# 64x64 tiles in a small self attention, and a band built by base-4 digits

## The chip, the cores and the metric

The kernel runs on one core of a Trainium2 chip. The metric is the device time of one execution in microseconds. A profiled execution adds a trace, from which the times of single instructions below are taken.

## The reference

A Perceiver of four levels: 2 batches of 64 latents with 256 features, beside a context of 2 x 1024 rows with 192 features. Each level has a cross attention to the context, a mixing of the latents among themselves, and a mixture of experts, each with a layer norm in front and a residual. All is float32. Two of the twelve stages are touched by the change.

Level 0's self attention has 8 heads of 64 features and one key and one value head that all share. It normalises its input a second time with gain and bias, and normalises its output:

```python
# xn: (2, 64, 256); q: 8 heads of 64; k, v: one head of 64
q = (xn @ Wq) * 64 ** -0.5
k, v = split(xn @ Wkv)
p = softmax(q_h @ k.T)            # per batch and head, 64 x 64
out = layer_norm(concat_h(p @ v) @ Wo)
```

Level 1's mixing gives each latent t a softmax over 32 taps, computed from its own features, and sums that latent and the 31 behind it by these weights:

```python
w = softmax(x @ W.T + b)          # (2, 64, 32)
# out[t] = sum over taps k of w[t, k] * x[t + k], rows past the end left out
```

As a matrix this is a band of 64 x 64 for each batch: row t holds its 32 weights, moved to the right by t.

## The kernel before

All 2 x 64 latents lie on the 128 partitions (batch 0 on the first 64, batch 1 on the others), and a stage works on a tile `x` of 128 x 256. The stages follow one another. Matmuls of f32 appear in the trace as two records each. Within the edited stages the program order holds on TensorE (PE), VectorE (DVE), ScalarE (ACT) and GpSimd: `in_written_order` chains each engine's instructions as they are written. So PE does nothing in a wait unless other work is written there.

That other work is the fill. Generators such as `kv1.keys(b, c)` and `kv1.values(b, t)` project the keys and values that a later cross attention needs; `steps(fill[k], n)` runs n steps of one of them. A step is a few matmuls (two of 512 columns for keys by `ctxA` in L413 and `ctxB` in L418, or four of 256 for values in L387 and L389); the last step is the eviction from PSUM, on ACT (L480, L483). PSUM is split into two pairs of banks (`two_banks`) and four single banks (`bank`), each used in a ring.

**Level 0's self attention (L1207 to L1287).** `xlT` is the normalised input, transposed. `kT` holds the keys twice, on partitions 0 to 63 and 64 to 127. The queries are laid out so that one 128 x 128 matmul gives a head's scores of both batches, with zeros in `qx` that keep the two heads of a chunk apart:

```python
for h in range(8):
    nc.tensor.matmul(sc[:, h, :], qx[:, h // 2, h % 2, :], kT, start=True, stop=True)
```

Of each 128 x 128 result only the two blocks where query and key are of one batch are used. They are copied to `l0a_s` (DVE L1248, ACT L1249), go through a softmax there, and come into `p`, a tile of 128 x 1024 that is zero elsewhere. Eight transposes (L252), eight matmuls with `v` (L1263), the division by the sum (L1265), four transposes of the result `o` and four matmuls with `wo` follow. Then come the statistics (`bn_st`, L1276), the output norm and the residual. Level 0's expert stage starts with a layer norm, the rest of the fill and the transposes of `xl`.

**Level 1's mixing (L1529 to L1582).** After the softmax (exponentials in L1555, division in L1558 and L1559) the 32 weights of each row have to move to the right by the row's number. Six steps do it, one for each binary digit: `bits[:, k]` is 1 in the rows whose number has digit k set and `unset` is its opposite; a step adds the row as it is times `unset` (L1571) to the row moved by 2^k times `bits` (L1574). The last step writes into the two diagonal blocks of `band`. One transpose, a copy to `bandT`, one matmul with `xl` (L1580) and the residual (L271) end it. Three fill pairs (L387 and L389) stand ahead of the transpose, one behind the matmul.

Weights come over the SyncE queue in written order, each load as its buffer comes free.

Of the kernel before, what the change touches and what calls it, by code (L numbers as in the profile page):

```python
# [8 lines left out]
F32 = mybir.dt.float32  # L9
# [3 lines left out]
AF = mybir.ActivationFunctionType  # L13
ALU = mybir.AluOpType
AX = mybir.AxisListType
# [3 lines left out]
P = 128  # L19
D = 256  # L20
NB = 2
# [37 lines left out]
def tile_perceiver(ctx: ExitStack, tc: tile.TileContext, i: dict, out: bass.AP):  # L59
# [28 lines left out]
    def bank():  # L88
        return psum_now["b"].tile([P, 512], F32, tag="b", name="bank")

    def two_banks():
        return psum_now["a"].tile([P, 1024], F32, tag="a", name="two_banks")

    def stat(n=1, name="stat"):
        return small.tile([P, n], F32, tag=f"s{n}", bufs=12 if n == 1 else 4, name=name)
# [103 lines left out]
    for k in range(6, -1, -1):  # L199
        bit = bits[:, k : k + 1]  # L200
        nc.vector.tensor_scalar(bit, place, float(1 << k), None, ALU.is_ge)
        nc.vector.scalar_tensor_tensor(place, bit, -float(1 << k), place, ALU.mult, ALU.add)
    nc.vector.tensor_scalar(unset, bits, -1.0, 1.0, ALU.mult, ALU.add)
    iota8 = const.tile([P, 8], F32, name="iota8")
    nc.gpsimd.iota(
        iota8, pattern=[[1, 8]], base=0, channel_multiplier=0,
# [53 lines left out]
    def accumulate(dst, pairs):  # L260
        for k, (lhsT, rhs) in enumerate(pairs):
            nc.tensor.matmul(dst, lhsT, rhs, start=(k == 0), stop=(k == len(pairs) - 1))  # L262
# [104 lines left out]
    def features(xT, w, at, n):  # L367

        ps = bank()
        for f in range(n):  # L370
            accumulate(
                ps[:, f * P : (f + 1) * P],
                [(w[:, c, (at + f) * P : (at + f + 1) * P], xT[:, c, :]) for c in range(2)],
            )
        return ps
# [109 lines left out]
    def steps(work, n=9):  # L485

        for _, _ in zip(range(n), work):
            pass
# [719 lines left out]
    with psum(2, 4), stage_pool(name="l0a", bufs=1) as pool, in_written_order():  # L1208
        wq, wkv, wo = weight("l0a_wq"), weight("l0a_wkv"), weight("l0a_wo")
        xl = layernorm(x, twice=True, then=AF.Exp)  # L1210
        xlT = pool.tile([P, 2, P], F32, name="l0a_xT")

        qx = pool.tile([P, 4, 2, P], F32, name="l0a_qx")
        nc.gpsimd.memset(qx, 0.0)
        p = pool.tile([P, 8, P], F32, name="l0a_p")
        nc.gpsimd.memset(p, 0.0)
        base = tok.tile([P, D], F32, tag="xb", name="x_bias")
        nc.gpsimd.tensor_tensor(base, x, row("l0a_ob"), ALU.add)
        steps(fill[1], 2)
        ps = bank()  # L1220
        for c in range(2):
            nc.tensor.transpose(ps[:, c * P : (c + 1) * P], xl[:, c * P : (c + 1) * P], ident)
        for c in range(2):
            evacuate_affine(
                xlT[:, c, :], ps[:, c * P : (c + 1) * P], col("l0a_w", c), col("l0a_b", c)
            )

        ps = features(xlT, wkv, 0, 1)
        kT = pool.tile([P, P], F32, name="l0a_kT")
        nc.scalar.copy(kT, ps[:, :P])  # L1230
        ps = features(xlT, wq, 0, 4)
        for h in range(2):
            r = slice(h * S, (h + 1) * S)
            nc.vector.tensor_scalar(
                qx[r, :, h, :], ps[r, :].rearrange("p (c t) -> p c t", c=4), 0.125, None, ALU.mult
            )
        steps(fill[0])
        ps = bank()
        accumulate(ps[:, :64], [(xlT[:, c, :], wkv[:, c, P:]) for c in range(2)])
        v = pool.tile([P, 64], F32, name="l0a_v")  # L1240
        nc.vector.tensor_copy(v, ps[:, :64])
        steps(fill[1], 1)
        sc = two_banks().rearrange("p (h t) -> p h t", h=8)
        for h in range(8):
            nc.tensor.matmul(sc[:, h, :], qx[:, h // 2, h % 2, :], kT, start=True, stop=True)

        s = pool.tile([P, 8, S], F32, name="l0a_s")
        nc.vector.tensor_copy(s[0:S], sc[0:S, :, 0:S])  # L1248
        nc.scalar.copy(s[S:P], sc[S:P, :, S:P])  # L1249
        mx, tot = stat(8, "l0a_mx"), stat(8, "l0a_tot")  # L1250
        nc.vector.tensor_reduce(mx, s, AX.X, ALU.max)
        nc.vector.tensor_tensor(s, s, mx.unsqueeze(2).to_broadcast([P, 8, S]), ALU.subtract)
        for b in range(NB):
            r = slice(b * S, (b + 1) * S)
            nc.scalar.activation(p[r, :, r], s[r], AF.Exp)
        nc.vector.tensor_reduce(tot, p, AX.X, ALU.add)
        nc.vector.reciprocal(tot, tot)
        steps(fill[1])
        steps(fill[2], 3)
        pT = transposed(p.rearrange("p h t -> p (h t)"), 8, pool, "l0a_pT", "l0a_pT")  # L1260
        ps = bank()
        for h in range(8):
            nc.tensor.matmul(ps[:, h * 64 : (h + 1) * 64], pT[:, h, :], v, start=True, stop=True)  # L1263
        o = pool.tile([P, 512], F32, name="l0a_o")
        nc.vector.tensor_tensor(  # L1265
            o.rearrange("p (h d) -> p h d", h=8), ps.rearrange("p (h d) -> p h d", h=8),
            tot.unsqueeze(2).to_broadcast([P, 8, 64]), ALU.mult,
        )
        steps(fill[2])
        oT = transposed(o, 4, pool, "l0a_oT", "l0a_oT")  # L1270
        ps = bank()
        accumulate(ps[:, :D], [(oT[:, c, :], wo[:, c, :]) for c in range(4)])
        steps(fill[3], 1)

        st, mv = stat(6, "bn_st"), stat(2, "bn_mv")
        nc.vector.bn_stats(st, ps[:, :D])  # L1276
        nc.vector.bn_aggr(mv, st)
        r = stat(name="rstd")
        nc.scalar.activation(r, mv[:, 1:2], AF.Sqrt, bias=eps, scale=1.0)
        y = pool.tile([P, D], F32, name="l0a_y")  # L1280
        nc.vector.scalar_tensor_tensor(
            y, ps[:, :D], mv[:, 0:1], row("l0a_ow"), ALU.subtract, ALU.mult
        )
        nc.vector.reciprocal(r, r)
        x_new = xpool.tile([P, D], F32, tag="x", name="x_new")
        nc.vector.scalar_tensor_tensor(x_new, y, r, base, ALU.mult, ALU.add)
        x = x_new  # L1287
# [247 lines left out]
    with psum(2, 4), stage_pool(name="l1a", bufs=1) as pool, in_written_order():  # L1535
        steps(fill[1], 1)
        xl = layernorm(x, then=AF.Exp)
        xlT = turned_rows(xl)
        ps = bank()
        accumulate(ps[:, :32], [(xlT[:, c, :], router("l1a", c)) for c in range(2)])  # L1540
        steps(fill[1])
        steps(fill[2], 2)


        PAD = 32
        skew = [pool.tile([P, PAD + S], F32, name=f"l1a_skew{k}") for k in range(2)]
        for t in skew:
            nc.gpsimd.memset(t, 0.0)
        band = pool.tile([P, P], F32, name="l1a_band")
        nc.gpsimd.memset(band, 0.0)  # L1550
        w = skew[0][:, PAD : PAD + 32]
        nc.vector.tensor_tensor(w, ps[:, :32], row("l1a_b"), ALU.add)
        nm, tot, ri = stat(name="l1a_nm"), stat(name="l1a_tot"), stat(name="l1a_ri")
        nc.vector.tensor_reduce(nm, w, AX.X, ALU.max, negate=True)
        nc.scalar.activation(w, w, AF.Exp, bias=nm, scale=1.0, accum_out=tot)  # L1555
        steps(fill[2])
        steps(fill[3], 1)
        nc.vector.reciprocal(ri, tot)  # L1558
        nc.vector.tensor_scalar(w, w, ri, None, ALU.mult)  # L1559
        width = 32  # L1560
        for k in range(6):
            src, far = skew[k % 2], 1 << k
            width = min(width + far, S)
            if k < 5:
                places = [(slice(0, P), skew[1 - k % 2][:, PAD : PAD + width])]
            else:
                places = [
                    (r, band[r, r]) for r in (slice(b * S, (b + 1) * S) for b in range(NB))
                ]
            for r, dst in places:  # L1570
                nc.vector.tensor_scalar(  # L1571
                    dst, src[r, PAD : PAD + width], unset[r, k : k + 1], None, ALU.mult
                )
                nc.vector.scalar_tensor_tensor(  # L1574
                    dst, src[r, PAD - far : PAD - far + width], bits[r, k : k + 1], dst,
                    ALU.mult, ALU.add,
                )
        bandT = transposed(band, 1, pool, "bandT", "bandT")
        ps = bank()
        nc.tensor.matmul(ps[:, :D], bandT[:, 0, :], xl, start=True, stop=True)  # L1580
        steps(fill[3], 1)
        x = residual(x, ps[:, :D])  # L1582


    with psum(2, 4), stage_pool(name="l1f", bufs=2) as pool:
# [701 lines left out]
def layout(inputs):  # L2287
# [55 lines left out]
    a["l0a_wq"] = rows_first(g[p + "Wq"])  # L2343
    kv = g[p + "Wkv"]
    a["l0a_wkv"] = rows_first(np.concatenate([kv[:, :64], kv], axis=1))
    a["l0a_wo"] = rows_first(g[p + "Wo"])
    p = "L0_ffn_"
    a["l0f_w"] = np.concatenate(
        [flat(rows_first(g[p + "w1"])), flat(rows_first(g[p + "w2"]))], axis=-1
# [98 lines left out]
```

## Time and profile before

| | us |
|---|---|
| three runs | 691.6, 693.4, 694.55 |
| median | 693.4 |
| profiled execution | 693.79 |
| its span in the trace | 692.1 |
| level 0's self attention, from the end of the q matmuls to `bn_stats` | 85.2 to 103.2 |
| level 1's mixing, from the exponentials to the residual's end | 188.1 to 195.3 |
| mean granted TensorE clock over the span | 0.995 |

The time of an execution is 1.7 us longer than its span. In lines of the trace the first number is the start in us from the span's start (in groups: the busy time), then comes the busy time, engine, line and operation, what was written and read, and the shape; in brackets, how long the engine was idle before and what ended that. PEld is the weight load of TensorE, which overlaps with its matmuls. The ends of matmuls are modelled.

### The profile page before, as it was taken

The numbers are of one execution on the slowest core, as the hardware profiler recorded it, in microseconds if no ns is written. First come the engines' busy times: TensorE is split into PE (matmuls) and PEld (weight loads), VectorE is DVE, ScalarE is ACT, GpSimd is POOL, SyncE is SP. The second block draws the span as 40 slices with busy tenths as digits, with TensorE's granted clock in tenths as the row PEclk, the third lists the DMA queues.
The fourth block names the chain that finished last, engine by engine and source line by source line (L and its number), as shares of the span: only waits on it lengthen the run. The fifth ranks groups of instructions, "written<-read, shape, count | busy, mean of one in ns | idle before, by whom it ended". The sixth has DMA issues, their size and how long they took to land.

```text
span 692.1 us, 12000 instructions
## 1 busy us (share of the span) xinstructions
PE 654.6 (95%) x4956; PEld 513.6 (74%) x4956; DVE 297.7 (43%) x794; ACT 262.8 (38%) x531; POOL 64.4 (9%) x90
## 2 busy tenths in 40 slices
PE   7989979999989999999998989999999999999997
PEld 3547658866669988999997778899979966754443
DVE  5875333267540014555553435535322267643111
ACT  2463433288553333323322515305231168532111
POOL 3440100000100000000000040120000000000340
PEclk9999989999999999999999999999999999999999
DMA  8950004840018877000002300021138820368981
GB/s 284 412 232 1 19 36 138 298 142 2 2 62 290 306 247 252 1 2 1 1 1 67 116 0 1 2 65 59 62 108 295 292 97 2 111 270 341 390 317 54
DMA packets 21365, 93.07 MB, mean 134 GB/s; under 512 B 3056, under 2 KB 7680, under 8 KB 12512
## 3 DMA queue, kind: packets, MB, share of 16 engines
q1 hardware_dynamic: 19040, 85.96, 33.9%
q0 software_dynamic: 2016, 6.30, 2.5%
q8 instruction: 39, 0.64, 0.4%
q14 instruction: 14, 0.11, 0.1%
q10 hardware_dynamic: 256, 0.06, 0.0%
HBM read 98.46 MB, written 0.13 MB: 142 GB/s over the span
## 4 chain that ended last, share of the span: by engine, by line
PE 88%; DVE 7%; ACT 2%; issue 1%; DMA 0%; DVEq 0%; ACTq 0%
PE bank L262 30%; PE bank L1708 6%; PE two_banks L620 5%; PE two_banks L1657 4%; PE bank L665 3%; PE two_banks L1359 3%; PE two_banks L1664 3%; PE two_banks L1384 2%; PE two_banks L1903 2%; PE two_banks L387 2%; PE bank L1384 2%; PE bank L1429 2%; PE bank L2023 2%; PE two_banks L413 2%; PE two_banks L262 1%
## 5 line engine op out<-in xcount | busy, mean ns | idle before, releaser
L1708 PE MATMUL bank<-l2x_ctx,p 128*128 128x193 f32 x256 | 48.1, 327 | 0.0
L362 DVE SCALAR_TENSOR_TENSOR x_new<-bank,comb,x_new 128x256 f32<-128x256 f32 x24 | 11.6, 484 | 80.0 <-PE bank L262 80.0
L1708 PEld LDWEIGHTS bank<-l2x_ctx,p 128*128 128x128 f32 x256 | 40.8, 191 | 0.4
L1369 DVE CUSTOM_DVE_ANT_0 p<-two_banks,zero 128x1024 f32<-128x1024 f32 x32 | 38.6, 1217 | 5.1 <-PE two_banks L1359 5.1
L1377 ACT ACTIVATE p<-p,negmax 128x1024 f32<-128x1024 f32 x32 | 36.9, 1153 | 4.6 <-DVE negmax L1369 4.6
L1657 PE MATMUL two_banks<-l2x_qA,ctxA 128*128 128x128 f32 x256 | 31.9, 278 | 0.0
L1657 PEld LDWEIGHTS two_banks<-l2x_qA,ctxA 128*128 128x128 f32 x256 | 30.3, 192 | 1.1 <-issue 1.0
L1672 DVE TENSOR_REDUCE l2x_mx<-two_banks 128x128 f32<-128x1024 f32 x16 | 19.6, 1224 | 26.3 <-PE two_banks L1664 26.3
L1598 ACT ACTIVATE l1f_hT<-bank,cols 128x128 f32<-128x128 f32 x64 | 18.2, 368 | 32.9 <-PE bank L262 32.9
L262 PEld LDWEIGHTS bank<-xT,l1f_w_sb 128*128 128x128 f32 x256 | 29.7, 192 | 0.6 <-issue 0.3
L262 PE MATMUL bank<-xT,l1f_w_sb 128*128 128x128 f32 x256 | 30.1, 276 | 0.0
L262 PEld LDWEIGHTS bank<-xT,l2f_w_sb 128*128 128x128 f32 x256 | 29.6, 192 | 0.3
L262 PE MATMUL bank<-xT,l2f_w_sb 128*128 128x128 f32 x256 | 29.8, 275 | 0.0
L262 PE MATMUL bank<-l1f_w_sb,l1f_hT 128*128 128x256 f32 x128 | 28.8, 379 | 0.0
L1694 DVE TENSOR_TENSOR p<-two_banks,l2x_shift 128x512 f32<-128x512 f32 x32 | 20.6, 686 | 13.3 <-ACT l2x_shift L1689 13.3
L262 PEld LDWEIGHTS bank<-l1f_w_sb,l1f_hT 128*128 128x128 f32 x128 | 23.8, 190 | 2.9
L1701 ACT ACTIVATE p<-p 128x512 f32<-128x512 f32 x32 | 19.6, 630 | 12.1 <-DVE p L1694 12.1
L1384 PEld LDWEIGHTS two_banks<-ident,p 128*128 128x128 f32 x128 | 13.7, 141 | 10.9 <-ACT pT L1413 9.1
L620 PE MATMUL two_banks<-l3f_w_sb,m_xg 128*64 128x512 f32 (+1 forms) x112 | 21.2, 595 | 0.5 <-ACT m_xg L643 0.5
L215 ACT ACT_TABLE_LOAD x16 | 20.5, 1283 | 0.3
L628 DVE TENSOR_TENSOR m_prod<-two_banks,m_g 128x512 f32<-128x512 f32 x10 | 6.9, 690 | 31.1 <-PE two_banks L620 31.1
L1359 PE MATMUL two_banks<-n_kT,n_qx 32*128 32x512 f32 x128 | 19.2, 640 | 0.0
(580 smaller groups left out, 1356.5 us busy)
## 6 DMA issues: line engine op xcount, KB each, us to landing
l1f_w_sb<-in_l1f_w_dram SPq DMA_DIRECT2D x16, 1024.0 KB, 5.1
l3f_w_sb<-in_l3f_w_dram SPq DMA_DIRECT2D x12, 1024.0 KB, 6.0
more_w<-in_l3f_w_dram SPq DMA_DIRECT2D x12, 1024.0 KB, 10.9
l0f_w_sb<-in_l0f_w_dram SPq DMA_DIRECT2D x8, 1024.0 KB, 8.5
l2f_w_sb<-in_l2f_w_dram SPq DMA_DIRECT2D x8, 1024.0 KB, 4.8
l2f_w_sb<-in_l2f_w_dram SPq DMA_DIRECT2D x8, 512.0 KB, 4.7
xh<-in_ctx_dram SPq DMA_DIRECT2D x8, 192.0 KB, 6.0
l2x_ctx<-in_ctx_dram SPq DMA_DIRECT2D x1, 1536.0 KB, 7.8
```

Source lines behind the costliest of these rows:

```text
L215: nc.scalar.activation(junk, behind, func, scale=0.0)
L262: nc.tensor.matmul(dst, lhsT, rhs, start=(k == 0), stop=(k == len(pairs) - 1))
L620: nc.tensor.matmul(part[s], xg[r][:, c, s], shelf.at[r, j, n](c, f), start=False, stop=(c == 1), skip_group_check=True,)
L665: nc.tensor.matmul(ps[s, :D], hT[r][:, f, s], shelf.at[r, j, 2](f, slice(0, D)), start=(f == 0), stop=(f == last),)
L1359: nc.tensor.matmul(sc[u][:, n * 512 : (n + 1) * 512], qx[c, n][rows_, b].rearrange("p h q -> p (h q)"), kT[c, b][rows_, n, :], start=True, ...
L1369: nc.vector.tensor_tensor_reduce(p[u], sc[u], zero.to_broadcast([P, NK]), -1.0, 3.0e38, ALU.add, ALU.min, least)
L1377: nc.scalar.activation(p[u], p[u], AF.Exp, bias=sc[u], scale=-1.0, accum_out=total[u // 4][:, u % 4 : u % 4 + 1],)
L1384: nc.tensor.transpose(ps[:, kc * P : (kc + 1) * P], p[u][:, (4 * k + kc) * P : (4 * k + kc + 1) * P], ident,)
L1657: nc.tensor.matmul(sc[k][:, n, t, :], ctxA[:, b, n, t * P : (t + 1) * P], qA[:, j, b].rearrange("p h q -> p (h q)"), start=(t == 0), stop= ...
L1664: nc.tensor.matmul(sc[k][:, n, t, :], ctxB[half[n], b, t * P : (t + 1) * P], qB[half[n], j, b].rearrange("p h q -> p (h q)"), start=False, ...
L1694: nc.vector.tensor_tensor(p[k][:, n], sc[k][:, n], shifts[k].unsqueeze(1).to_broadcast([P, 4, P]), ALU.add,)
L1708: nc.tensor.matmul(po[k][:, : CD + 1], p[k][:, kc // 4, kc % 4, :], crows[:, b * 8 + kc, :], start=(kc == 0), stop=(kc == 7),)
```

## The change

In level 0's self attention the matmuls work on single 64 x 64 blocks: scores of one head and one batch, and the sum over values of one head and one batch. The queries stay as `features` gives them, in two halves. The values come onto four blocks (`v`, 128 x 128). Scores of the even heads go to one PSUM bank and those of the odd heads to another, so that the softmax needs no copy and is done in two halves of 128 x 256. The weights are divided by their sum before the transposes, one half on GpSimd and one on DVE. The matmul with `v` gives its result transposed already, so `o` and its transposes are gone; `wo`'s rows are reordered in the layout to suit. The memsets of `qx` and `p` are gone. Of the fill, `fill[1]`'s `ctxB` step stands behind the scores, `fill[2]`'s `ctxB` step behind `wo`, and its eviction behind the square root of the output norm.

In level 1's mixing rows move in three steps, one for each digit to the base of four: a multiplication of four shifted readings of the row with `digit` (products of `bits` and `unset`, made once at the start on GpSimd), and a reduction over the four. The blocks are turned by two 64 x 64 matmuls with `ident`; ACT and DVE copy one each into `bandT`. The division by the sum moves into the last addition. One of the three fill pairs moves behind the matmul with `xl`.

```diff
+    digit = const.tile([P, 3, 4], F32, name="digit")
+    low, high = (
+        [t[:, :6].rearrange("p (k u) -> p k u", u=2)[:, :, u] for t in (bits, unset)]
+        for u in range(2)
+    )
+    for j in range(4):
+        nc.gpsimd.tensor_tensor(digit[:, :, j], low[j % 2], high[j // 2], ALU.mult)
...
-        qx = pool.tile([P, 4, 2, P], F32, name="l0a_qx")
-        nc.gpsimd.memset(qx, 0.0)
-        p = pool.tile([P, 8, P], F32, name="l0a_p")
-        nc.gpsimd.memset(p, 0.0)
...
+        for j in range(2):
+            ps = features(xlT, wq, 2 * j, 2)
+            dst = qT[j].rearrange("p c t -> p (c t)")
+            if j == 0:
+                nc.vector.tensor_scalar(dst, ps[:, :D], 0.125, None, ALU.mult)
+                steps(fill[0])
+            else:
+                nc.scalar.activation(dst, ps[:, :D], AF.Identity, scale=0.125)
+        own = [slice(b * S, (b + 1) * S) for b in range(NB)]
         ps = bank()
-        accumulate(ps[:, :64], [(xlT[:, c, :], wkv[:, c, P:]) for c in range(2)])
...
+                    nc.tensor.matmul(
+                        ps[own[n], own[b]], xlT[:, c, own[b]], wkv[:, c, P:],
+                        start=(c == 0), stop=(c == 1),
+                    )
...
+        sc = [bank() for g in range(2)]
+        for c in range(4):
+            for b in range(NB):
+                for g in range(2):
+                    nc.tensor.matmul(
+                        sc[g][own[b], c * S : (c + 1) * S],
+                        qT[c // 2][own[g], c % 2, own[b]], kT[own[g], own[b]],
+                        start=True, stop=True,
+                    )
+        for g in range(2):
+            s, mx = sc[g][:, : 4 * S].rearrange("p (c k) -> p c k", c=4), stat(4, "l0a_mx")
+            nc.vector.tensor_reduce(mx, s, AX.X, ALU.max)
+            nc.vector.tensor_tensor(
+                p[g], s, mx.unsqueeze(2).to_broadcast([P, 4, S]), ALU.subtract
+            )
+            nc.scalar.activation(p[g], p[g], AF.Exp)
+        for g in range(2):
+            tot = stat(4, "l0a_tot")
+            nc.vector.tensor_reduce(tot, p[g], AX.X, ALU.add)
+            nc.vector.reciprocal(tot, tot)
+            engine = nc.vector if g else nc.gpsimd
+            engine.tensor_tensor(
+                weights[g], p[g], tot.unsqueeze(2).to_broadcast([P, 4, S]), ALU.mult
+            )
         steps(fill[1])
-        steps(fill[2], 3)
+        steps(fill[2], 2)
...
+            po = [bank() for n in range(2)]
+            for b in range(NB):
+                for n in range(2):
+                    nc.tensor.matmul(
+                        po[n][own[n], :D].rearrange("p (m t) -> p m t", m=2)[:, :, own[b]],
+                        v[own[n], own[b]], pT[g][own[n], :, own[b]], start=True, stop=True,
+                    )
+            nc.scalar.copy(oT[g][own[0]].rearrange("p m t -> p (m t)"), po[0][own[0], :D])
+            nc.vector.tensor_copy(oT[g][own[1]].rearrange("p m t -> p (m t)"), po[1][own[1], :D])
...
-        steps(fill[2])
-        oT = transposed(o, 4, pool, "l0a_oT", "l0a_oT")
...
+        steps(fill[2], 1)
         steps(fill[3], 1)
...
         nc.scalar.activation(r, mv[:, 1:2], AF.Sqrt, bias=eps, scale=1.0)
+        steps(fill[2])
...
+        for k, n in enumerate(steps_of):          # 1, 4, 16
+            width = min(width + 3 * n, S)
...
+            nc.vector.tensor_tensor(
+                terms, four, digit[:, k].unsqueeze(1).to_broadcast([P, width, 4]), ALU.mult
+            )
+            dst = rows_of if k == 2 else moved[k + 1][:, 12 * n : 12 * n + width]
+            nc.vector.tensor_reduce(dst, terms, AX.X, ALU.add)
...
+            nc.tensor.matmul(
+                turned[b][own[b], :S], rows_of[own[b]], ident[own[b], own[b]],
+                start=True, stop=True,
+            )
         nc.vector.reciprocal(ri, tot)
-        nc.vector.tensor_scalar(w, w, ri, None, ALU.mult)
...
-        steps(fill[3], 1)
-        x = residual(x, ps[:, :D])
+        steps(fill[3], 2)
+        x_new = xpool.tile([P, D], F32, tag="x", name="x_new")
+        nc.vector.scalar_tensor_tensor(x_new, ps[:, :D], ri, x, ALU.mult, ALU.add)
```

## The prediction

> **What bounds it now.** I read the page's 40 slices first, then the granted clock in short stretches, then the timeline of the two stages that are edited.
>
> ```profile
> PE   7989979999989999999998989999999999999997
> PEclk9999989999999999999999999999999999999999
> PE 88%; DVE 7%; ACT 2%; issue 1%; DMA 0%; DVEq 0%; ACTq 0%
> ```
>
> TensorE (PE) carries 88% of the chain that ended last and DMA none of it, so time comes off only where PE does less, or where PE idles. Both edits sit in such places: the sixth slice (86 to 104 us: busy 7, clock 8), and the eleventh and twelfth (173 to 208 us: busy 9 and 8). The list of waits names no DMA as what PE waited for, and weight loads start as buffers come free, so what is gained here should stay gained.
>
> ```profile
> 94.60:98.00 3.40, 2.27 (x19) 2.14 (x19) 0.98 (x2) 2.55 (x4) 0.00 (x0) 1.00 0.00 0
> 98.00:101.40 3.40, 2.62 (x9) 1.86 (x8) 0.69 (x1) 0.00 (x0) 0.00 (x0) 0.50 0.02 5
> 101.40:104.80 3.40, 3.40 (x9) 2.23 (x7) 1.41 (x5) 0.29 (x1) 0.00 (x0) 0.50 0.18 36
> ```
>
> In these stretches (busy time of PE, weight loads, DVE, ACT, POOL, then the clock) PE runs at half clock from 98.0 to 104.8 us, after a stretch of thin work. It is the only fall of the clock in this trace, and it doubles the matmuls by `wo`.
>
> ```profile
> 86.57 2.05 PE L1245 MATMUL two_banks<-l0a_kT,l0a_qx 128*128 128x128 f32 x16
> 88.66 0.68 DVE L1248 COPY l0a_s<-two_banks 64x512 f32<-64x512 f32 x1 [1.70 <-PE two_banks L1245]
> 89.37 0.58 ACT L1249 COPY l0a_s<-two_banks 64x512 f32<-64x512 f32 x1 [4.45 <-DVE l0a_s L1248]
> 89.99 0.69 DVE L1251 TENSOR_REDUCE l0a_mx<-l0a_s 128x8 f32<-128x512 f32 x1 [0.65 <-ACT l0a_s L1249]
> 91.49 1.28 ACT L1255 ACTIVATE l0a_p<-l0a_s 64x512 f32<-64x512 f32 x2 [1.54 <-DVE l0a_s L1252]
> 94.94 2.00 PE L1263 MATMUL bank<-l0a_v,l0a_pT 128*128 128x64 f32 x16 [0.87 <-DVE l0a_pT L103]
> 97.73 0.89 PE L252 MATMUL bank<-ident,l0a_o 128*128 128x128 f32 x4 [0.79 <-DVE l0a_o L1265]
> 99.40 3.78 PE L262 MATMUL bank<-l0a_wo_sb,l0a_oT 128*128 128x256 f32 x8 [0.79 <-DVE l0a_oT L103]
> 103.22 0.43 DVE L1276 BATCH_NORM_STATS2 bn_st<-bank 128x6 f32<-128x256 f32 x1 [3.87 <-PE bank L262]
> ```
>
> Level 0's attention is a serial chain: each row waits for the one above. From the end of the q matmuls (85.2) to the end of `wo` (103.2) it takes 18.0 us.
>
> **Level 0, part by part.** An f32 matmul is two records. Nothing in this trace has 64 rows and 64 columns of the array at once. The nearest rows:
>
> ```profile
> 74.54 0.45 PE L1097 MATMUL bank<-l0x_uT,l0x_wv 96*64 96x64 f32 x8
> 74.82 0.29 PE L1097 MATMUL bank<-pT,vl 128*64 128x64 f32 x4
> 75.04 1.12 PE L418 MATMUL two_banks<-ctxB,l1x_wk_sb 64*128 64x512 f32 x2
> ```
>
> Twelve records with halves of the columns in turn take 75.04 - 74.54 = 0.50 us, 42 ns each. Bounds: 34 ns (L1429, 32 records in 1.08 us) and 125 ns (L1263, 16 in 2.00 us). I take 42, as the shape is nearest, and 61 ns for the 16 records with 128 moving columns (half of L262's 1.95 us / 16 = 122 ns, two tiles in turn). After a group's last issue I add 0.2 us to its result.
>
> - Values: 16 records x 42 ns = 0.67, against 0.38 before; 85.2 to 85.9.
> - Scores: 32 x 42 = 1.34 + 0.2, done at 87.4. They now stand ahead of the fill (`ctxB`, 1.06 us) that ran before them. The second half of q is copied by ACT behind two 0.63 us key evictions (83.66 to 84.92), so at 85.6, before the scores need it.
> - Softmax on DVE: two times reduce and subtract at 0.42 (128x256: 0.415 in L1837, 0.425 in L1845), with gaps 1.85; 89.25. Both PSUM-to-SBUF score copies (0.68 + 0.58) are gone, and the exponentials (0.42 each) lie beside the other half's DVE work, apart from the last.
> - Sum 0.42, reciprocal 0.16, multiplication: GpSimd 0.72 (L1218's 0.723 for 128x256), about 1.4 with gaps: 90.65 for half 0; on DVE half 1 is ready at 91.0. Before, the sum over 1024 columns took 1.22, but beside PE.
> - PE meanwhile has 1.06 + 1.9 us of fill (`ctxB`, `ctxA`): 87.2 to 90.2, so it idles about 0.5. If that fill were not there, these 3 us would be idle and paid later.
> - Four transposes (0.13 each) in place of eight, evicted at 0.37 (ACT) and 0.42 (DVE): 91.9. ACT's two key evictions (1.26) come first, 89.7 to 90.9, just clear.
> - Weighing: 16 x 61 ns = 1.0, its first half overlapping the eviction: done 92.5. The copies of 64x256 (0.37 ACT, 0.42 DVE) end at 93.15 for half 1. The normalisation of the output (L1265, 0.69), the four transposes of `o` (0.89) and their copy (0.69) are gone.
> - `wo`: 2.1 us at full clock (L262's 1.13 for two matmuls, twice, less one drain), its first half ahead of the last copy: done at 94.8.
>
> So `bn_stats` starts at 94.8 instead of 103.2, 8.4 us earlier, of which 1.65 + 0.35 is the half clock on `wo` and on the transposes of `o`. After that PE holds the end, not the normalisation: fill of 1.06 (moved here) + 3.4 (two pairs of L387 and L389, 1.06 + 0.63 each) ends at 99.1, while `xl` is ready at 98.3 (3.5 us after `bn_stats`, as 106.7 - 103.2 before). The key eviction that now follows the square root on ACT (1.26 us) ends about when the next root needs ACT. The transposes of `xl` start at 99.1 instead of 107.14: **8.0 us**.
>
> The two memsets of 0.95 us on GpSimd stood off the path and give nothing. The four `digit` products on GpSimd are free: GpSimd is idle until 13.13 us, and `unset` is ready at 8.6. If that cover were gone they would cost about 0.6 (four at 0.14, L205's kind).
>
> **Level 1's mixing.**
>
> ```profile
> 188.54 0.16 DVE L1558 RECIPROCAL l1a_ri<-l1a_tot 128x1 f32<-128x1 f32 x1 [0.54 <-ACT l1a_skew L1555]
> 193.49 0.30 PE L252 MATMUL bank<-ident,l1a_band 128*128 128x128 f32 x1 [1.04 <-DVE l1a_band L1574]
> 194.18 0.70 PE L1580 MATMUL bank<-xl,bandT 128*128 128x256 f32 x2 [0.38 <-DVE bandT L103]
> 197.14 0.41 PE L252 MATMUL bank<-ident,xl 128*128 128x128 f32 x2 [0.77 <-DVE xl L238]
> ```
>
> From 188.54 to 193.34 DVE runs sixteen small instructions of 0.16 to 0.28 us. In their place are three multiplications and three reductions of 140, 188 and 256 elements: 2 x (0.30 + 0.355 + 0.42) + six gaps of 0.04 = 2.4, ending at 190.95. Whether the strided reads cost more: L1672 reduces 1024 strided elements in 1224 ns and L1256 1024 contiguous ones in 1220, so nothing; at worst the three multiplications double, +1.1. The reciprocal runs beside the turn on PE. PE is through with its two fill pairs at 190.76. The turn takes 0.3, DVE's copy ends at 191.6, but ACT's copy of the other block stands behind the eviction of `n_v` (190.80, 1.01 us): 192.05. `bandT` x `xl` starts at 192.1, 2.1 us earlier. Then the third fill pair, moved behind it, is late next: 0.5 + two pairs (3.4) end at 196.0, while `xl` would be ready at 195.0. Transposes at 196.0 instead of 197.14: **1.1 us** of the 2.1.
>
> **Sum.** The profiled execution is 693.79 us (span 692.1 + 1.7 around it), 0.4 above the median of 693.4. 693.8 - 8.0 - 1.1 = 684.7. I don't shift it to the median: how much half clock an execution catches may well be what spreads the three times over 2.95 us, and the new time has none in it.
>
> [...] By the trace, half clock came without any PE gap over 1.0 us in 92 to 98. [...]
>
> [...]
>
> **Rivals.**
> - *The clock falls again.* About 89.5 to 93 PE has some 2.0 of 3.4 us busy, no more than the 2.27 that preceded the fall. Against it: 87.8 to 91.2 (2.01) and 190.8 to 194.2 (1.98) stayed at 1.00. One or two windows of 3.4 us at half clock cost 1.7 to 3.4, as PE then holds the end: 686.4 to 688.1.
> - *Small tiles do not run in turn.* At 125 ns instead of 42 for 48 records, +4.0, and 122 for 61 on 16, +1.0: 689.7. For it: a smaller tile still loads its weights per record; against it: L1097's pace.
> - *Slower: tiles of one bank drain one another.* If each of the 68 small records (16 + 32 + 16, and 4 in the mixing) waited for the one before, at the 246 ns of L1097's mean, that is 68 x 0.2 = 13.9 more: 698.6. It decides from about 180 ns a record on (9.1 us / 68 + 42 ns); L1097's pace speaks against it.
> - *The mixing gains nothing* since strided reads double (+1.1): 685.8.
>
> **Numbers.** Forecast as summed, 0.55 (own range 682.8 to 686); clock falls again 0.23; small tiles slow 0.10; mixing gains nothing 0.08; drain 0.04. The range 682.5 to 688.8 holds the first, second and fourth and leaves out most of the tile cases. What a measurement can tell here is about 0.5%, 3.5 us: within it lies only the upper part of the tile case, 0.06; slower 0.04; faster 0.90.
>
> **What would show it.** Right: `bn_st` of level 0 at 94 to 96 us, `wo` in about 2.1 us, PE continuous from `wo` to the transposes of `xl`; score records 35 to 50 ns apart; the six DVE instructions of the mixing in 2.4 us, and the second fill pair, not DVE, ahead of the level 1 expert stage. Wrong: clock 0.50 anywhere in 90 to 100 us; scores longer than 2.5 us; multiplications over 0.5 us; an end after 690 us.

## The result, and the profile after

The changed kernel takes 682.83 us (median of four runs, 682.35 to 683.42). The kernel before took 692.94 on the same chip (691.6 to 694.55). The ratio is 0.9854, with an interval of 0.9834 to 0.9875. The profiled execution took 683.42 us, with a span of 681.7. The forecast for it was 684.7, with a range of 682.5 to 688.8.

The page of the changed kernel, the three lines that answer to those of before:

```profile
PE   7989999999899999999998989999999999999997
PEclk9999999999899999999999999999999999999999
PE 89%; DVE 6%; ACT 3%; issue 1%; DMA 0%; POOL 0%; ACTq 0%; DVEq 0%; POOLq 0%
```

TensorE carries the chain as before. In the row of the clock the 8 has left the sixth slice, that of the attention, and stands in the eleventh, that of the mixing. The two edited stages in one view each, first before, then after. Its columns are the stretch, its length, the busy time of PE, weight loads, DVE, ACT and POOL, then the granted clock. A stretch runs from the transposes of one `xl` to those of the next.

```profile
81.45:107.14 25.69, 21.30 (x106) 14.51 (x106) 10.27 (x21) 10.46 (x18) 0.00 (x0) 0.87 0.14 47
185.90:197.14 11.24, 8.54 (x42) 5.11 (x42) 6.72 (x25) 5.06 (x9) 0.00 (x0) 1.00 0.01 2
```

```profile
79.96:96.53 16.57, 15.60 (x126) 9.59 (x127) 8.34 (x24) 10.76 (x21) 0.61 (x1) 1.00 0.21 73
175.38:186.86 11.48, 10.01 (x44) 5.96 (x45) 5.18 (x16) 5.87 (x11) 0.00 (x0) 0.85 0.01 2
```

The attention went from 25.69 to 16.57 us and PE is now busy in 15.60 of them, all at full clock. The mixing did not get shorter in this execution: part of it ran at half clock (0.85 on the mean). And the attention's stage already begins 1.49 us earlier (79.96 instead of 81.45), ahead of anything that was edited except the four small products on GpSimd. The whole difference of the spans, 10.4 us, is 1.49 ahead of the attention, 9.12 in it and -0.24 in the mixing; all the rest adds less than 0.1.

The attention's chain in the timeline of the changed kernel:

```profile
84.24 0.69 PE L1260 MATMUL bank<-l0a_kT,l0a_qT 64*64 64x64 f32 x32
84.86 1.13 PE L426 MATMUL two_banks<-ctxB,l1x_wk_sb 64*128 64x512 f32 x4
84.98 0.42 DVE L1269 TENSOR_REDUCE l0a_mx<-bank 128x4 f32<-128x256 f32 x1 [0.34 <-PE bank L1260]
87.37 0.61 POOL L1279 TENSOR_TENSOR l0a_w<-l0a_p,l0a_tot 128x256 f32<-128x256 f32 x1 [8.39 <-DVE l0a_tot L1277]
90.19 1.97 PE L270 MATMUL bank<-l0a_wo_sb,l0a_oT 128*128 128x256 f32 x8 [0.17 <-ACT l0a_oT L1307]
92.19 0.43 DVE L1318 BATCH_NORM_STATS2 bn_st<-bank 128x6 f32<-128x256 f32 x1 [1.67 <-PE bank L270]
96.53 0.44 PE L260 MATMUL bank<-ident,xl 128*128 128x128 f32 x2
```

The q matmuls end at 83.69, so the chain to `bn_st` takes 8.5 us where it took 18.0. `wo` takes 1.97 us instead of 3.78. The 32 records of the scores fill only 0.62 us (84.24 to the next group's start at 84.86): 19 ns each. The row of `xl`'s transposes has no idle time in front: PE works through its fill up to there, while `xl` was ready at 95.66.

### The profile page after: what moved, and what is told of

Its sections match the earlier page's. It is cut to its first block, busy times and chain, and to the rows that moved or that the text cites. A ratio compares the mean times of both kernels' runs of the same rounds, so it can differ in the third digit from the quotient of the medians.

```text
span 681.7 us, 12046 instructions
## 1 busy us (share of the span) xinstructions
PE 648.9 (95%) x4979; PEld 509.1 (75%) x4979; DVE 294.0 (43%) x788; ACT 263.2 (39%) x534; POOL 64.3 (9%) x94
## 4 chain that ended last, share of the span: by engine, by line
PE 89%; DVE 6%; ACT 3%; issue 1%; DMA 0%; POOL 0%; ACTq 0%; DVEq 0%; POOLq 0%
PE bank L270 30%; PE bank L1757 6%; PE two_banks L628 5%; PE two_banks L1706 4%; PE bank L673 3%; PE two_banks L395 3%; PE two_banks L1713 3%; PE two_banks L1402 2%; PE two_banks L1427 2%; PE two_banks L1952 2%; PE bank L1427 2%; PE bank L1472 2%; PE bank L2072 2%; PE two_banks L397 2%; PE two_banks L421 2%; PE two_banks L270 1%
## 5 line engine op out<-in xcount | busy, mean ns | idle before, releaser
L1721 DVE TENSOR_REDUCE l2x_mx<-two_banks 128x128 f32<-128x1024 f32 x16 | 19.6, 1224 | 26.5 <-PE two_banks L1713 26.5
## 6 DMA issues: line engine op xcount, KB each, us to landing
more_w<-in_l3f_w_dram SPq DMA_DIRECT2D x12, 1024.0 KB, 10.4
```

## The experiments

The theory: both stages got shorter by their chains, as forecast, and half clock is a separate matter that comes and goes with the execution. The rivals: the gain of the attention is mainly the clock; small tiles have a price that other work hides; the mixing's edit is worth nothing or less. The first four kernels ran on one chip, where the kernel before took 694.19 us (median of 23 runs), the last four on another, where it took 693.4 (9 runs).

**Level 0's part alone.** The mixing and its fill steps are those of before; `digit` is gone.

```diff
 # beside the changed kernel: L204-211 and L1588-1631 as before
...
-            nc.vector.tensor_reduce(dst, terms, AX.X, ALU.add)
...
+                nc.vector.scalar_tensor_tensor(
+                    dst, src[r, PAD - far : PAD - far + width], bits[r, k : k + 1], dst,
+                    ALU.mult, ALU.add,
+                )
```

> Level 0's part alone, the mixing as before. Stage lengths are taken from the transposes of one xl to those of the next: level 0's attention took 25.69 us before and 16.57 in the changed kernel. Theory (this part carries nearly the whole gain, by a shorter chain and a clock that stays up): attention stage 16.4 to 16.8 us, clock 1.00 in it, and 9 us of the time, so about 684 against 693; the mixing stage stays at 11.2. Rival (the two parts gain about alike, and some of what the profiles show is the clock's start at the head of the kernel, 1.5 us earlier there): 686 or more.

```profile
80.29:96.86 16.57, 15.60 (x126) 9.59 (x127) 8.35 (x24) 10.74 (x21) 0.61 (x1) 1.00 0.21 73
175.72:187.43 11.71, 10.07 (x41) 5.87 (x42) 6.42 (x24) 5.31 (x10) 0.00 (x0) 0.85 0.01 2
```

Measured: 687.55 us (685.41 to 689.95, six runs), ratio 0.9914 (0.9889 to 0.994), that is 6.0 us less by the ratio. In the trace the attention takes 16.57 us, to the hundredth what it takes in the changed kernel, and the mixing 11.71, with half clock in 177.5 to 181.0. So the 9.1 us of the stage are there without the other edit, as the theory had it, but the time gives back some 3 us of them, as the rival had it (686 or more). All six runs show a mean clock below 0.998 (four 0.997, one 0.994, one 0.992), where seven of the nine runs of the changed kernel show 0.999 or 1.0. The clock is thus part of what is missing, but two of the runs at 0.997 differ by 2.3 us, and a share is left over (see below what stays open).

**Level 1's part alone.** The attention is that of before.

```diff
 # beside the kernel before: the mixing and `digit` of the change
...
-        nc.vector.tensor_scalar(w, w, ri, None, ALU.mult)
...
+        nc.vector.scalar_tensor_tensor(x_new, ps[:, :D], ri, x, ALU.mult, ALU.add)
```

> The mixing's part alone, level 0's attention as before. The mixing stage took 11.24 us before; in the changed kernel 11.48, with 3.4 us of it at half clock. Theory: where no clock falls there the stage takes about 10.2 us and the time falls by 1.0 to 1.2 us, too little to be told from nothing in the time alone; attention stage 25.7 with a fall of the clock in it. Rival (the new mixing is no faster in itself: strided multiplications, the copy behind the eviction and the fill pair behind the matmul eat it): stage 11.2 or more at full clock, time as before.

Measured: 693.09 us (twelve runs), ratio 0.9986 (0.9973 to 0.9999): 1.0 us less, between 0.1 and 1.9. In its trace no half clock falls into the mixing:

```profile
185.26 0.44 PE L260 MATMUL bank<-ident,xl 128*128 128x128 f32 x2 [0.68 <-DVE xl L246]
191.54 0.67 PE L1592 MATMUL bank<-xl,bandT 128*128 128x256 f32 x2 [0.52 <-DVE bandT L1590]
195.33 0.44 PE L260 MATMUL bank<-ident,xl 128*128 128x128 f32 x2
```

From 185.26 to 195.33 the stage takes 10.07 us, 1.17 less than the 11.24 of before. The matmul with `bandT` starts 6.28 us into the stage; before it was 8.28 (194.18 - 185.90). Of the 2.0 us won there 1.17 reach the end. The forecast's 2.1 and 1.1 hold.

**The kernel before with PE kept busy.** How much of the attention's gain is clock? `keep_busy(n)` issues n matmuls of 128 x 256 whose result nobody reads. Three of them go into each of three waits of the old attention.

```diff
 # attention of the kernel before; around the weighing and the transposes of o
+        keep_busy(3, ps)
...
-        oT = transposed(o, 4, pool, "l0a_oT", "l0a_oT")
+        oT = pool.tile([P, 4, P], F32, tag="l0a_oT", name="l0a_oT")
...
+        keep_busy(3, ps)
...
+        keep_busy(3, ps)
```

> The kernel before, with three matmuls that nobody reads (128x256, ones) ahead of the weighing, ahead of the transposes of o, and ahead of wo, each written into the PSUM bank that the next step overwrites: PE idles less between 94 and 99.4 us and nothing else changes. Theory (thin PE work in one clock window makes the clock fall, at a cost of about 2.4 us): clock 1.00 throughout the stage, wo in about 2.1 us instead of 3.78, attention stage 23.3 instead of 25.69, time 690.5 to 691. Rival (the fall has another cause, or costs nothing since the chain waits anyway): clock 0.50 again, or the time as before or slower by the added matmuls.

```profile
80.61:104.73 24.12, 21.70 (x124) 16.07 (x125) 10.27 (x21) 10.15 (x18) 0.00 (x0) 1.00 0.15 50
```

```profile
97.88 1.46 PE L303 MATMUL bank<-ctxA,ones 128*128 128x256 f32 x6
99.17 1.89 PE L262 MATMUL bank<-l0a_wo_sb,l0a_oT 128*128 128x256 f32 x8
```

The clock of the stage is 1.00 now (0.87 before), and `wo` takes 1.89 us where it took 3.78. The stage takes 24.12 us, 1.57 less than before. The added groups of 1.46 us are longer than the waits they fill: `wo`'s input was there at 98.77 and `wo` began at 99.17, and the weighing and the transposes of `o` began late in the same way, by 0.32 and 0.46; in the profile of before each of the three begins 0.05 or 0.06 after its input. Without these delays, 1.0 us more than before in all, the stage would be an estimated 2.6 us shorter than before. So of the 9.1 us that the change won, between 1.6 and 2.6 are half clock and the rest, 6.5 to 7.5, is the shorter chain. The time is 692.72, where 690.5 to 691 was expected; the ratio is 0.9984 (0.9969 to 0.9998), a gain of 1.1. One reason stands in the trace: with the attention at full clock, half clock came in the mixing instead (185.4 to 188.9), and that stage took 11.75 us (183.46 to 195.21) where it took 11.24 before.

**The same tile in a row.** The scores' loops are nested the other way, so that four matmuls follow one another on one 64 x 64 tile.

```diff
-        for c in range(4):
-            for b in range(NB):
-                for g in range(2):
+        for b in range(NB):
+            for g in range(2):
+                for c in range(4):
```

> The changed kernel with its 16 score matmuls in another order: four of one 64x64 tile in a row, then the next tile, where the changed kernel goes to another tile with each. The changed kernel's 32 score records take 0.62 us, 19 ns each. Theory (tiles of the array run beside one another, so the pace comes from taking them in turn): 40 to 70 ns a record, 1.3 to 2.2 us for the scores, attention stage longer by 0.7 to 1.5 us. Rival (64x64 records are simply short, 19 ns is what one costs): pace and stage unchanged.

```profile
84.70 1.54 PE L1260 MATMUL bank<-l0a_kT,l0a_qT 64*64 64x64 f32 x32
86.17 1.13 PE L426 MATMUL two_banks<-ctxB,l1x_wk_sb 64*128 64x512 f32 x4
```

The 32 records take 1.47 us (84.70 to 86.17), 46 ns each instead of 19. The stage takes 17.10 us, 0.53 more, of the 0.85 that the scores take longer. The time is 685.56, a single run, and no run of the changed kernel stands beside it in that session. So the order makes the pace: 32 records that change tile each time follow one another in 19 ns, four in a row on one tile in 46. Each half of the array's rows writes to its own PSUM bank in both orders, so that taking turns over tiles and taking turns over banks are not told apart here.

**The changed kernel again, and three edits of its mixing.** The changed kernel itself, run once more:

> The changed kernel once more, beside the same runs of the kernel before as the next one. Level 0's part alone gave 0.9914 of the time before and the mixing alone 0.9986; if the two simply add up, this gives 0.990, 687 us beside 694. Theory (the parts add up in the stages, 9.1 and 1.2 us, and the rest is how many windows of 3.4 us run at half clock: the new mixing lets the clock fall less often than the old one once level 0 keeps it up): 0.985 to 0.987, and most runs with at most one fall. Rival (the first measurement was lucky): 0.989 to 0.991.

```profile
179.28 0.47 DVE L1608 TENSOR_TENSOR l1a_terms<-l1a_moved,digit 128x188 f32<-128x188 f32 x1
180.23 0.58 DVE L1608 TENSOR_TENSOR l1a_terms<-l1a_moved,digit 128x256 f32<-128x256 f32 x1
```

Measured: 682.6 us (682.44 to 683.75, five runs), ratio 0.9857 (0.9839 to 0.9875). The profile of this run has no half clock in the mixing, and the stage takes 10.14 us (175.82 to 185.96). So 1.34 us of the first profile's 11.48 are the half clock. In that first profile the fill ahead of the turn took longer (1.58, 1.22 and 1.73 us for its first three groups, where this run has 1.11, 0.70 and 1.13), so that the eviction of `n_v` came later and got in front of ACT's copy:

```profile
181.88 1.01 ACT L491 COPY n_v<-two_banks 128x1024 f32<-128x1024 f32 x1 [3.88 <-PE two_banks L397]
182.78 0.20 ACT L1624 COPY bandT<-bank 64x64 f32<-64x64 f32 x1
```

The first edit changes the layout of `terms`, so that the multiplications read and write along rows.

```diff
-                tensor=first.tensor, offset=first.offset, ap=[first.ap[0], [1, width], [n, 4]]
+                tensor=first.tensor, offset=first.offset, ap=[first.ap[0], [n, 4], [1, width]]
...
-            terms = pool.tile([P, S, 4], F32, name="l1a_terms")[:, :width]
+            terms = pool.tile([P, 4, S], F32, name="l1a_terms")[:, :, :width]
...
-                terms, four, digit[:, k].unsqueeze(1).to_broadcast([P, width, 4]), ALU.mult
+                terms, four, digit[:, k].unsqueeze(2).to_broadcast([P, 4, width]), ALU.mult
...
-            nc.vector.tensor_reduce(dst, terms, AX.X, ALU.add)
+            nc.vector.tensor_reduce(dst, terms.rearrange("p j w -> p w j"), AX.X, ALU.add)
```

> The changed kernel with the mixing's products laid out as four rows of the whole width, so that the multiplication reads and writes neighbours in order and the reduction strides instead. The three multiplications took 0.30, 0.46 and 0.58 us where 140, 188 and 256 elements of the nearest rows gave 0.30, 0.355 and 0.42. Theory (the step of 4 and 16 elements in what the multiplication reads costs the difference): 0.30, 0.355, 0.42 and reductions as before; the mixing stage hardly shorter, at most 0.1 us, since ACT's copy behind the eviction is then last. Rival (another cause, such as the broadcast operand): 0.46 and 0.58 again; or the reductions grow by as much.

```profile
180.38 0.43 DVE L1608 TENSOR_TENSOR l1a_terms<-l1a_moved,digit 128x256 f32<-128x256 f32 x1
180.84 0.59 DVE L1612 TENSOR_REDUCE l1a_rows<-l1a_terms 128x64 f32<-128x256 f32 x1
```

The multiplications now take 0.30, 0.35 and 0.43 us instead of 0.30, 0.47 and 0.58, and the reductions 0.39, 0.47 and 0.59 instead of 0.30, 0.35 and 0.42. The price has moved from the one to the other and grown a little, as the first step's reduction is strided too. The reductions have no broadcast operand, and they grew by as much, so the stride and not the broadcast is what costs. The six instructions end 2.84 us after their start, against 2.79 in the first profile. Half clock fell into the mixing (178.5 to 181.9) and the stage took 11.48 us, as in the first profile. One run took 683.98 us.

The second edit moves the eviction of `n_v` behind the two copies to `bandT`.

```diff
-        steps(fill[2])
...
         nc.vector.tensor_copy(bandT[own[1], own[1]], turned[1][own[1], :S])
+        steps(fill[2])
```

> The changed kernel with the eviction of n_v on ACT written behind ACT's copy of its band block instead of ahead of it. Theory (at full clock the eviction ends just as the turned block is there, so nothing waits for it, and only a fall of the clock made it late): with no fall in the mixing the stage stays within 0.1 us of 10.07; with a fall in the same place as in the changed kernel the band's matmul starts 0.5 us earlier. Rival (the copy behind the eviction holds the matmul): 0.4 us or more shorter at full clock.

```profile
182.84 0.23 DVE L1624 COPY bandT<-bank 64x64 f32<-64x64 f32 x1 [0.46 <-PE bank L1618]
182.88 1.00 ACT L491 COPY n_v<-two_banks 128x1024 f32<-128x1024 f32 x1
```

The stage takes 10.14 us (176.86 to 187.00), the same as without the edit. At full clock the eviction is through by the time that the turned blocks are there (in the second run of the changed kernel it ends at 181.74, and the two copies begin at 181.74 and 181.80), so its place costs nothing. At half clock it did cost: there the eviction began at 181.88 and ACT's copy came 0.55 us after DVE's. This run took 683.57 us without any half clock, because its attention began at 81.45, as late as in the kernel before.

The third kernel has both edits and one `keep_busy` on either side of the transposes of `xl` ahead of the mixing.

```diff
+        keep_busy(1, ps)
+        for c in range(2):
+            nc.tensor.transpose(ps[:, c * P : (c + 1) * P], xl[:, c * P : (c + 1) * P], ident)
...
+        keep_busy(1, ps)
```

> The changed kernel with the products in rows, the eviction behind the band, and two matmuls that nobody reads (128x256, ones) in the mixing's two waits ahead of the router, where PE idles 0.5 to 0.7 us each. Theory (thin work around the layer norm makes the clock fall in some runs, at 1.2 us each): no fall between the transposes and the end of the mixing in any profile, clock 0.999 or 1.000 in most runs, stage 9.7 to 9.9 us, and the time 0.5 to 1.2 us below the changed kernel's in the same session. Rival (falls come from elsewhere, or the added matmuls delay the chain by what they save): clocks 0.997 as before, time equal or longer.

Measured: 682.42 us (five runs), ratio 0.9851 (0.9833 to 0.9869). The mixing took 10.19 us, not the 9.7 to 9.9 expected, and no half clock fell into it. The changed kernel itself, on the same chip, has it in only one of its five runs by the mean clock (0.997), so there was little to save, and 682.42 can't be told from 682.6. None of the three beats the changed kernel.

## Why the prediction was right, and where it was off

The forecast was 684.7 for the profiled execution, and it took 683.42: 1.28 less. Three terms make this up: the attention won 1.1 more than forecast, the head of the kernel 1.49 that no step spoke of, and the half clock in the mixing took 1.34 back. That the last two nearly cancel is luck. The run with the eviction moved had neither, as its attention began at 81.45 and its clock never fell; it took 683.57, and of its distance to the forecast the attention's 1.1 is nearly all.

**The attention: mechanism right, the scores mis-sized.** The stage was forecast at -8.0 and came to -9.1. The step that failed is "32 x 42 = 1.34 + 0.2". The 32 records took 0.62 us, and DVE's first reduction began 1.29 us after the end of the q matmuls, where 2.2 was forecast. The lower bound of 34 ns was too high as well. The row that I chose has two halves of the columns in turn; here four tiles take turns, and the run with the same tile in a row shows that the turns are what sets the pace: 19 ns against 46. The softmax gave another 0.3 (from that reduction to the end of half 1's multiplication, at 88.25, 3.27 us, forecast 3.6). Values (0.62, forecast 0.67), GpSimd's multiplication (0.61, forecast 0.72) and `wo` (1.97, forecast 2.1) were sized well. The drain that the sum for `wo` takes off is shown by no run; what the kernel before shows is a group of two such matmuls that takes 1.13 us (L262 at 77.99) while the next group begins 0.97 after its start (78.96). From `bn_st` to the transposes 4.3 us were forecast and 4.34 came: PE's fill holds the end, and `xl` is ready 0.9 us before. Of the signs that the prediction named, PE's continuous work from `wo` to these transposes came; `bn_st` at 92.19 and 19 ns a record lie below the ranges given.

**The clock in the attention.** That `wo` loses its half clock came true; keeping PE busy in the old kernel gives the same 1.9 us for `wo`. The rival "the clock falls again" was placed in the stretch from 89.5 to 93 with an estimated 2.0 us busy of 3.4. That was wrong: PE was busy for 3.12 of 3.41 us in 88.47 to 91.88, as the small matmuls lie close together.

**The mixing: right without half clock.** The forecast of -1.1 is what the undisturbed stage shows (10.07 and 10.14 against 11.24). Two steps in it were off and small. The multiplications were forecast at 0.30, 0.355 and 0.42 and took 0.30, 0.47 and 0.58: the strided reads cost 0.27 us together, where the sum had nothing and the bound 1.1. With the gaps the six instructions took 2.79 us instead of 2.4, and the third multiplication, over 0.5, is a sign that the prediction had named for being wrong. The row that I argued from, L1672 (1224 ns for 1024 elements), strides as these do but reads PSUM (`two_banks`), while these tiles lie in SBUF; that difference was overlooked, and no run shows whether it is the cause. Then the rival did arrive here: half clock from 177.3 to 180.7 cost 1.34 us in the first profile. The forecast had seen only that the window from 190.8 had stayed at full clock in the kernel before.

The run with the terms in rows sizes the strides: the step that reads neighbours costs nothing extra (0.30 in both layouts), and the two that read every fourth and every sixteenth element take 0.12 and 0.15 more than along rows (0.47 against 0.35, 0.58 against 0.43), some 0.6 ns for each of their 188 and 256 elements. Why a stride costs this is not shown.

**The head, which no step spoke of.** The two `wlkv` rows and the first projections of the context, before and then after:

```profile
7.74 3.78 PE L262 MATMUL bank<-l0x_wlkv_sb,latT 128*128 128x512 f32 x4
11.31 1.70 PE L387 MATMUL two_banks<-wkc,ctxA 128*128 128x256 f32 x4
```

```profile
7.53 3.22 PE L270 MATMUL bank<-l0x_wlkv_sb,latT 128*128 128x512 f32 x4
10.59 1.03 PE L395 MATMUL two_banks<-wkc,ctxA 128*128 128x256 f32 x4
```

The same matmuls are slow for longer in the kernel before: the pace of these rows doubles at about 12.7 us there and at about 10.1 here (worked out from how much of each group ran at each pace). It is not the change, since the run with the eviction moved, which has all of the change, started its attention at 81.45 again. So 1.49 of the 10.4 us between the two spans is the luck of the two executions, and not to be counted for the edits. The forecast left out that a profile of before can begin unluckily.

**The rivals on the small tiles** fell. Tiles that do not run in turn were priced at 125 ns a record; even four in a row on one tile took 46 each. Tiles that wait for one another were priced at 246; the groups of 64 x 64 stood at 19, with no visible gap ahead of the next group (84.24, then 84.86).

**What stays open.** Alone, the two parts won 0.86 and 0.14 per cent, 1.0 together; both at once won 1.46, and 1.43 when repeated on the second chip. The traces of the stages add up, the times don't: what is missing is in level 0's part, whose runs caught more half clock than those of the changed kernel. Why the old mixing should draw it more often is not shown. The profile of level 0's part also loses 1.0 us in level 3's expert stage, which no edit touches: PE idles 0.94 us there, between 640 and 650 us, and what it waits for is not shown. All four profiles from the first chip have such a wait at this place (PE 0.3 to 1.0 late), the other six have none. The kernel before was not profiled on the first chip; if it waits there too, this cancels in the ratio.

## What to carry to other kernels

Where a stage is a serial chain on an engine that is else always busy, cost it by the distance from one engine's last result to the next's first instruction, then ask whether PE's remaining work or the chain arrives last; that gave both stages to within 1.1 us. With small tiles, order the loops so that consecutive matmuls lie on different tiles, since here this order set the price of a record (19 against 46 ns). Before a difference of a few microseconds between two profiles is put down to an edit, compare the start of the edited stage and the granted clock in both.

## What was unexpected of the hardware

Half clock comes in pieces of 3.41 to 3.42 us: one in five of the profiles, two in a row (6.83) in two, worked out from the granted clock in stretches of 0.25 and 0.5 us. By their distances they lie on a grid, and the doubling of the pace at the head lies on it too. Before, the pace doubles at 12.7 us and half clock begins at 98.0, 85.3 us or 25 x 3.41 later. After, it doubles at 10.1 and half clock begins at 177.3, 167.2 us or 49 x 3.41 later. Seven of the ten profiles have a fall ahead of the kernel's last 3 us, and in their traces' records of the clock it begins 25 (two profiles), 49 (four) or 51 (one) such pieces after the doubling. How little PE does just ahead does not decide it alone:

```profile
173.60:177.00 3.40, 2.21 (x14) 1.24 (x13) 1.68 (x6) 2.74 (x5) 0.00 (x0) 1.00 0.00 0
177.25:180.25 3.00, 3.00 (x10) 1.59 (x9) 2.08 (x7) 0.42 (x2) 0.00 (x0) 0.51 0.01 3
```

PE is busy for 2.21 of 3.40 us, and then the clock halves. In the second run of the same kernel the same stretch has the same 2.21, and the clock stays at 1.00. Nor is a thin piece of the grid enough: in the kernel before, the piece from 87.8 us on lies 22 x 3.41 after the doubling, PE is busy for 2.01 of 3.40 us in it, and the clock stays at 1.00. So in all seven profiles the fall came behind a thin piece (PE busy for 2.2 to 2.3 of 3.41 us), but what else decides is not shown.

Of the 23 runs of the kernel before on the first chip, three with a mean clock of 1.0 take 691.08 to 692.05 us, eleven with 0.994 take 693.7 to 694.64 and three with 0.992 take 695.11 to 695.55. The other six (0.993 to 0.999) take 691.88 to 695.17 and do not all follow that order. One piece more at half clock is 0.0025 of the mean (half of 3.41 us in 692) and, by an estimate from the first two groups, about 1.2 us. This and the head's 1.5 can make up much of the 4.5 us over which these runs spread; no run takes the two apart.

At the head, the profile's granted clock reads 1.00 (7.0 to 10.0 us of the kernel before) while the matmuls run at half pace: 0.89 us for each of the four records of 128 x 512 from 7.74 to 11.31, where L1034's four from 55.21 to 56.93 take 0.43 each. The durations have to be read there, not the clock.
